# Attention units in another order: a unit's exponentials in the next unit, both halves of its squares amid that unit's score instructions, results copied out between the exponentials

## The chip, the core and the metric

The kernel runs on one core of a Trainium2 chip. The core has TensorE (matrix products; PE in the profile, and PEld for its weight loads), VectorE (DVE), ScalarE (ACT), GpSimd (POOL) and SyncE (SP, which here only issues DMAs). The metric is device time in microseconds for one execution; the median of the runs is compared.

## What is computed

Two images of 48 x 48 positions with 768 channels pass through two layers. The first is group norm, attention with decomposed relative position bias, and a projection; the second is group norm and a spectral mixing layer. The change lies in the attention of the first. Per head (12 heads of 64 channels, S = 2304 positions), cut from the reference:

```python
attn = einsum('bqc,bkc->bqk', q * scale, k)
rel_h = einsum('bhwc,hkc->bhwk', r_q, Rh); rel_w = einsum('bhwc,wkc->bhwk', r_q, Rw)
attn = softmax(attn + rel_h[..., :, None] + rel_w[..., None, :])
out = attn @ v            # then out @ proj_w + proj_b, added to x
```

All of it is float32.

## The kernel before, in words

`block_kernel` works on one image after the other: `attention`, then `project_out`, then `Spectral`. In `attention` the heads go in six pairs, both heads of a pair side by side on the partitions. The queries of a pair are cut into 18 *units* of 128 queries: six groups g, each with x = 0, 1, 2 (`order`, L481). In each iteration n of the loop (L502) the work of several units is interleaved by hand; the engines are wrapped so that every instruction keeps its place in the program (`InOrder`, L60: therefore most lines of the profile are L68). Each engine runs its own queue in that order.

One unit goes through these steps:

- `new_unit` (L346, POOL): two adds, one for each head, build the bias `s` (128 x 2304 for each head) from `rhw`, which holds the rows of the relative bias for a whole group. `s` has four buffers.
- `scores` (L360): five pieces of keys (four of 512, one of 256) by two heads, ten matmuls on TensorE into banks `ps_s`. For each, VectorE adds the product into `s` and keeps the maximum (the CUSTOM_DVE rows); then it reduces the maxima to `nm`.
- `numerators` (L389, ScalarE): four exponentials, two halves of the keys by two heads, with sums in `parts`.
- `squares` (L403, VectorE): two transposes in 32 x 32 blocks for a half, one for each head.
- `exchange` (L409): per half, six DMAs on SP's queue and two copies on ScalarE gather the blocks into `pT` (two buffers).
- `weigh` (L423): 72 matmuls on TensorE multiply `pT` with the values, into the one bank `ps_o`.
- `finish` (L440): ScalarE copies `ps_o` into `res`, VectorE sums `parts` into `dens`; at x = 2 SP stores `res`. `inverses` (L458) turns the `dens` of half a pair and sends them.

Around it stands the work that fills TensorE: in each unit of pairs 0 to 4 one piece of the next pair's keys or values (x = 0, 1) or of queries (x = 2), evicted by ScalarE (keys, queries: `by_act`) or VectorE (values: `by_dve`). Pair 5 has no next pair, so its units at x = 0 and 1 have none. The weights `w` for these come by `load_w` (L194) on SP's queue, in an iteration with x = 2 for values and keys.

The bias of a group is made ahead. At x = 2 the queries of the group after the next are projected (`queries`). One iteration later, at x = 0, `relative` (L295) multiplies them with the tables into two banks `ps_r`; ScalarE copies these to `rel`; `write` sends `rel` to DRAM with a skew (two DMAs), and `read` fetches it back straightened, as `rhw` (two DMAs). `new_unit` for that group's x = 0 unit comes two iterations after `relative`.

All banks but `ps_o` come from one pool of seven, in a ring.

The loop's order before, for iteration n (unit n is `un`, n - 1 is `last`, n - 2 is `older`): scores of un, numerators of un, a projection, weigh of older, `relative`, the evictions of ScalarE, squares and exchange of last's second half, `write`, squares and exchange of un's first half, the evictions of VectorE, `read`, finish of older, `new_unit` for n + 1.

Of the kernel before, what the change touches and what calls it, by code (L numbers as in the profile page):

```python
# [17 lines left out]
P = 128  # L18
# [144 lines left out]
def attention(tc, k, x_b, a, oT, inv_d, late, span, ps_b, ps_o):  # L163
# [12 lines left out]
    with ExitStack() as ctx:  # L176
# [65 lines left out]
        def evict(waiting):  # L242
            while waiting:
                waiting.pop(0)()
# [50 lines left out]
        def relative(g, qT):  # L295

            row0 = min(32, 40 - 8 * g)  # L300
            both = [bank(f"ps_r{h}") for h in range(2)]
            for x in range(3):
                for h in range(2):
                    r = slice(h * HD, (h + 1) * HD)
                    rows = k.rel[r, row0 : row0 + RW]
                    step = REL + 32 - 16 * x - row0
                    pe.matmul(
                        both[h][:, x * 2 * RW : (x + 1) * 2 * RW],
                        lhsT=qT[r, x, :],
                        rhs=bass.AP(rows.tensor, rows.offset, [rows.ap[0], [step, 2], [1, RW]]),  # L310
                        start=True,
                        stop=True,
                    )
            for h in range(2):
                dst = rel[:, :, :, h, :].rearrange("p k x j -> p x k j")
                src = both[h][:, :ROW].rearrange("p (x k j) -> p x k j", x=3, k=2)
                by_act.append(lambda dst=dst, src=src: act.copy(dst, src))

            rhw = qp.tile([P, 3, 2, 2 * HW], F32, tag="rhw", name="rhw")
            t_ds = []  # L320

            def write():
                for kind in range(2):
                    t_d = dp.tile([P * RS + 16], F32, tag=f"t{kind}", name=f"t{kind}")
                    t_ds.append(t_d)
                    skew = [[16 * RS + 1 - kind, 8], [RS + kind, 16], [1, ROW]]
                    sync.dma_start(
                        out=bass.AP(t_d.tensor, t_d.offset, skew),
                        in_=rel[:, kind].rearrange("p x h j -> p (x h j)"),
                    )  # L330

            def read():
                for kind, first in enumerate((47 - 8 * g - row0, 15)):
                    t_d = t_ds[kind]
                    sync.dma_start(
                        out=rhw[:, :, :, kind * HW : (kind + 1) * HW].rearrange(
                            "p x h j -> p (x h) j"
                        ),
                        in_=bass.AP(
                            t_d.tensor, t_d.offset + first, [[RS, P], [RW, 6], [1, HW]]  # L340
                        ),
                    )

            return rhw, write, read
# [11 lines left out]
            return {"pr": pr, "g": g, "x": x, "qT": qT, "s": s}  # L356

        PIECES = [(k0, min(S, k0 + 512)) for k0 in range(0, S, 512)]

        def scores(un):  # L360

            mx = smallp.tile([P, 2, len(PIECES)], F32, tag="mx", name="mx")
            for j, (k0, k1) in enumerate(PIECES):
                both = [bank(f"ps_s{h}") for h in range(2)]
                for h in range(2):
                    r = slice(h * HD, (h + 1) * HD)
                    pe.matmul(
                        both[h][:, : k1 - k0],
                        lhsT=un["qT"][r, un["x"], :],
                        rhs=kTs[un["pr"]][r, k0:k1],  # L370
                        start=True,
                        stop=True,
                    )
                for h in range(2):
                    s = un["s"][:, h, k0:k1]
                    dve.tensor_tensor_reduce(
                        out=s,
                        in0=both[h][:, : k1 - k0],
                        in1=s,
                        scale=1.0,  # L380
                        scalar=LOWEST,
                        op0=ALU.add,
                        op1=ALU.max,
                        accum_out=mx[:, h, j : j + 1],
                    )
            un["nm"] = smallp.tile([P, 2], F32, tag="nm", name="nm")
            dve.tensor_reduce(un["nm"], mx, AX.X, ALU.max, negate=True)

        def numerators(un):  # L389

            un["parts"] = smallp.tile([P, 2, 2], F32, tag="parts", name="parts")
            for half in range(2):
                for h in range(2):
                    s = un["s"][:, h, half * 2 * KQ : (half + 1) * 2 * KQ]
                    act.activation(
                        s,
                        s,
                        AF.Exp,
                        bias=un["nm"][:, h : h + 1],
                        accum_out=un["parts"][:, h, half : half + 1],  # L400
                    )

        def squares(un, half):  # L403

# [35 lines left out]
        def finish(un):  # L440

            pr, g, x = un["pr"], un["g"], un["x"]
            if x == 0:
                outs[pr, g] = outp.tile([P, 8, 3, 16], F32, tag="res", name="res")
                if g % 3 == 0:
                    dens[pr, g // 3] = outp.tile([P, 3, 2, 3], F32, tag="dens", name="dens")
            res = outs[pr, g]
            act.copy(res[:, :, x, :], un["o"][:, :P].rearrange("p (y d) -> p y d", d=16))
            dve.tensor_reduce(
                dens[pr, g // 3][:, x, :, g % 3], un["parts"], AX.X, ALU.add  # L450
            )
            if x == 2:
                sync.dma_start(
                    out=oT[pr * P : (pr + 1) * P, g * UQ : (g + 1) * UQ],
                    in_=res.rearrange("p y x d -> p (y x d)"),
                )
# [40 lines left out]
        weights[2] = load_w(2, 0)  # L497
        staged = ((0, 1), queries(0, 1))
        evict(by_act)
        recent = []  # L500
        last = turn = send = None
        for n in range(len(order) + 3):  # L502
            un = older = None
            if n < len(order):
                un = ahead
                pr, g, x = order[n]
                if g == 4 and x == 0 and pr + 1 < NP:
                    weights[0] = load_w(0, pr + 1)
                scores(un)
                recent.append(un)  # L510
            write = read = None
            if un is not None:
                numerators(un)
                ready, staged = staged, None
                if x == 2:
                    if n + 4 < len(order):
                        key = order[n + 4][:2]
                        staged = (key, queries(*key))
                    if g == 2 and pr + 1 < NP:
                        weights[2] = load_w(2, pr + 1)  # L520
                    if g == 5 and pr + 2 < NP:
                        weights[1] = load_w(1, pr + 2)
                elif n < 2:
                    for i in range(3):
                        values(0, 3 * n + i)
                    if n:
                        weights[1] = load_w(1, 1)
                elif pr + 1 < NP:
                    i = 2 * g + x
                    for j in range(0 if n == 3 else i, i + 1):  # L530
                        (keys if j < 6 else values)(pr + 1, j % 6)
            if turn is not None:
                turn()
                turn = None
            if n >= len(order) - 1 and recent:
                late(n - len(order) + 2)
            if n > 1 and recent:
                older = recent.pop(0)
                weigh(older)
            if un is not None and ready is not None:  # L540
                key, qT = ready
                rhw, write, read = relative(key[1], qT)
                groups[key] = (qT, rhw)
            evict(by_act)
            if last is not None:
                squares(last, 1)
                exchange(last, 1)
            if write is not None:
                write()
            if un is not None:  # L550
                squares(un, 0)
                exchange(un, 0)
            evict(by_dve)
            if read is not None:
                read()
            if older is not None:
                finish(older)
            if un is not None and n + 1 < len(order):
                ahead = new_unit(*order[n + 1])
            if send is not None:  # L560
                send()
                send = None
            if older is not None and older["x"] == 2 and older["g"] % 3 == 2:
                turn, send = inverses(older["pr"], older["g"] // 3)
            if len(order) - 6 <= n <= len(order):
                late()
            last = un


def shifts(t):  # L570
# [660 lines left out]
```

## Time and profile before

| | us |
|---|---|
| median of 3 runs (3729.47 to 3737.5) | 3736.94 |
| the profiled execution | 3736.53 |
| its span, first to last instruction | 3734.3 |
| TensorE busy (95%) | 3558.8 |
| VectorE busy (78%) | 2914.9 |
| ScalarE busy (68%) | 2544.2 |
| POOL busy (55%) | 2046.2 |

The profiled execution's time is 2.2 us longer than its span. The busy times are sums over the whole span. The granted TensorE clock has a mean of 0.978 of full speed. In the page's part 5 a row is a group of like instructions, with busy time, mean length of one, and the idle time of the engine just before them with what ended it. A timeline shows start, length, engine, line, operation and count of instructions in order of time; what stands in brackets is idle time before them and what ended it. In busy times by windows, each engine's busy time in a stretch stands with the count of its instructions in brackets, then the granted clock, the DMA engines' busy share and GB/s.

### The profile page before, as it was taken

How to read it: one execution, taken by the hardware profiler on the slowest of the kernel's cores; microseconds unless marked ns; L12 is line 12 of the kernel's file. 1: busy time of each engine (PE TensorE's matmuls, PEld its weight loads, DVE VectorE, ACT ScalarE, POOL GpSimd, SP SyncE). 2: the span in 40 equal slices, each digit the busy share in tenths (PEclk: the TensorE clock that was granted, in tenths of full speed). 3: DMA queues.
4: the chain of work that ended last, by engine and by line, in shares of the span. 5: the costliest groups of instructions: out<-in, count | busy, mean ns of one | idle time of the engine just before them, and what ended most of it. 6: DMA issues, size and time to landing. Idle time of an engine off the chain costs nothing.

```text
span 3734.3 us, 92576 instructions
## 1 busy us (share of the span) xinstructions
PE 3558.8 (95%) x36032; PEld 2485.7 (67%) x36032; DVE 2914.9 (78%) x6788; ACT 2544.2 (68%) x3740; POOL 2046.2 (55%) x662
## 2 busy tenths in 40 slices
PE   8999999999999888989989999999999998879899
PEld 5677776767767655566566777767677676545665
DVE  4799998989999983347657999989998999933476
ACT  3788888888888882133237888888888888821432
POOL 2566757576766663413225667575757666644232
PEclk9999999999999998999989999999999999989999
DMA  3687777778787888634526877777787778886434
GB/s 103 151 181 170 178 174 174 177 167 184 169 180 168 177 190 189 170 95 120 163 77 151 181 171 176 176 172 178 168 184 168 179 169 181 196 188 160 103 112 137
DMA packets 497859, 607.61 MB, mean 163 GB/s; under 512 B 180493, under 2 KB 312973, under 8 KB 497422
## 3 DMA queue, kind: packets, MB, share of 16 engines
q1 hardware_dynamic: 497422, 601.69, 69.0%
q8 instruction: 286, 4.69, 0.6%
q14 instruction: 151, 1.24, 0.1%
HBM read 131.61 MB, written 87.67 MB: 59 GB/s over the span
## 4 chain that ended last, share of the span: by engine, by line
PE 82%; DVE 6%; DMA 4%; ACT 4%; issue 2%; POOL 1%; SPq 1%; ACTq 0%; DVEq 0%; POOLq 0%
PE ps_o L68 21%; PE ps_s L68 20%; PE ps_proj L68 14%; PE acc L68 8%; PE ps_v L68 7%; DVE s L68 3%; PE ps L967 2%; PE ps_u L1002 2%; PE ps_y L727 2%; PE ps_r L68 2%; DMA pT<-s 2%; PE ps_x L1020 1%; SPq L68 1%; ACT pT L68 1%; PE ps_z L907 1%
## 5 line engine op out<-in xcount | busy, mean ns | idle before, releaser
L350 POOL TENSOR_TENSOR s<-rhw 128x2304 f32<-128x2304 f32 x432 | 1740.2, 4061 | 1066.8 <-DMA pT<-s 639.7
L68 DVE CUSTOM_DVE_ANT_0 s<-ps_s,s 128x512 f32<-128x512 f32 (+1 forms) x2160 | 1222.3, 633 | 312.3 <-issue 182.1
L68 ACT ACTIVATE s<-s,nm 128x1152 f32<-128x1152 f32 x864 | 1074.6, 1245 | 346.2 <-DVE nm L68 332.4
L68 DVE STREAM_TRANSPOSE s<-s 128x1152 f32<-128x1152 f32 x864 | 1111.9, 1344 | 5.5 <-ACT s L68 5.5
L68 ACT COPY pT<-s 32x1152 f32<-32x1152 f32 x864 | 993.4, 1150 | 21.7 <-PE ps_o L68 3.9
L68 PE MATMUL ps_o<-pT,v 128*64 128x128 f32 x15552 | 909.7, 277 | 65.1 <-ACT res L68 32.5
L68 PEld LDWEIGHTS ps_o<-pT,v 128*64 128x64 f32 x15552 | 877.8, 139 | 111.9 <-ACT res L68 55.8
L68 PE MATMUL ps_s<-kT,qT 64*128 64x512 f32 (+1 forms) x4320 | 899.0, 555 | 4.4 <-DVE mx L68 3.8
L68 PEld LDWEIGHTS ps_s<-kT,qT 64*128 64x128 f32 x4320 | 430.3, 187 | 418.9 <-issue 350.9
L68 PE MATMUL ps_proj<-xnT,w 128*64 128x384 f32 (+1 forms) x4032 | 589.6, 446 | 2.3 <-ACT gn_rstd L151 2.3
L68 PEld LDWEIGHTS ps_proj<-xnT,w 128*64 128x64 f32 x4032 | 280.8, 137 | 274.7 <-issue 216.9
L748 DVE TENSOR_TENSOR x<-acc,x 32x384 f32<-32x384 f32 (+2 forms) x216 | 119.2, 553 | 277.5 <-PE acc L68 194.7
L68 PE MATMUL acc<-proj 128*128 128x384 f32 x864 | 288.4, 493 | 40.8 <-POOL proj L68 40.8
L68 PE MATMUL ps_v<-w,xnT 128*64 128x128 f32 x5184 | 301.3, 276 | 0.0
L68 PEld LDWEIGHTS ps_v<-w,xnT 128*64 128x64 f32 x5184 | 285.9, 138 | 21.5 <-DVE mx L68 21.5
L68 PEld LDWEIGHTS acc<-proj 128*128 128x128 f32 x864 | 166.1, 193 | 157.5 <-POOL proj L68 41.6
L734 ACT COPY y<-ps_y 112x384 f32<-112x384 f32 x96 | 45.9, 478 | 265.8 <-PE ps_y L727 264.6
L68 POOL TENSOR_TENSOR proj<-proj 128x2304 f32<-128x2304 f32 x12 | 60.6, 5047 | 219.1 <-DMA proj<-inv_d 180.7
L68 DVE DVE_READ_ACCUMULATOR2_ANT mx<- 128x1 f32 x2160 | 179.4, 83 | 0.0
L984 POOL TENSOR_TENSOR spectrum<-spectrum 128x480 f32<-128x480 f32 x80 | 96.2, 1202 | 119.1 <-DVE spectrum L983 90.6
L68 ACT ACTIVATION_READ_ACCUMULATOR s<-s,nm 128x1 f32 x864 | 161.2, 187 | 0.0
L967 PE MATMUL ps<-w,spectrum 96*64 96x96 f32 x3200 | 143.1, 248 | 0.0
(106 smaller groups left out, 2107.1 us busy)
## 6 DMA issues: line engine op xcount, KB each, us to landing
pT<-s SPq DMA_DIRECT2D x2592, 144.0 KB
t<-rel SPq DMA_DIRECT2D x144, 189.0 KB
rhw<-t SPq DMA_DIRECT2D x144, 144.0 KB
y<-y_d SPq DMA_DIRECT2D x40, 360.0 KB
u_d<-spectrum SPq DMA_DIRECT2D x40, 360.0 KB
u<-u_d SPq DMA_DIRECT2D x48, 300.0 KB
xt<-in_x SPq DMA_DIRECT2D x12, 1152.0 KB
w<-in_qkv_w SPq DMA_DIRECT2D x36, 384.0 KB
```

The source lines that it names most:

```text
L68: return lambda *args, **kw: self.tc.keep_in_program_order(op(*args, **kw))
L350: nc.gpsimd.tensor_tensor(s[:, h, :].rearrange("p (y x) -> p y x", x=HW), rhw[:, x, h, :HW][:, :, None].to_broadcast([P, HW, HW]), rhw[:, ...
L727: nc.tensor.matmul(ps[:YP, : 2 * SC], lhsT=k.fw, rhs=part[:, t0 : t0 + 2, ch], start=True, stop=True,)
L734: nc.scalar.copy(y1[:, :, ch], ps[:YP, : 2 * SC].rearrange("p (t c) -> p t c", c=SC))
L748: nc.vector.tensor_tensor(dst, acc[p : p + n, :UQ], dst, ALU.add)
L907: nc.tensor.matmul(ps[:BS, w * 96 : (w + 1) * 96], lhsT=self.y2[s, j][:, w, i * BS : (i + 1) * BS], rhs=k.fh, start=True, stop=True,)
L967: nc.tensor.matmul(ps[64 * r : 64 * r + 64, w * BS : (w + 1) * BS], lhsT=self.o1[:, ri, f0 : f0 + 64], rhs=w2[:, (0, 2, 1, 0)[2 * r + ri], ...
L984: nc.gpsimd.tensor_tensor(val, val, clip, ALU.subtract)
L1002: nc.tensor.matmul(ps[: 2 * HW, :480], lhsT=k.ih, rhs=d2[:, c0 : c0 + 480], start=True, stop=True)
L1020: nc.tensor.matmul(ps[: 2 * HW, : 2 * SC], lhsT=k.iw, rhs=self.u2[s, i][:, t : t + 2, :], start=True, stop=True,)
```

## The change

For iteration n there are now four units in work: `un` = n, `last` = n - 1, `older` = n - 2 and `weighed` = n - 3. The new order is: numerators of last, first half; finish of weighed; `write` (with the two `rel` copies of ScalarE, which stood in `relative` before); numerators of last, second half; scores of un, pieces 0 to 2; squares and exchange of last, both halves; `read`; scores of un, pieces 3 and 4, with the reduction to `nm`; then the loads and the projection, weigh of older, `relative`, the evictions, `new_unit`. `write` and `read` belong to the `relative` of the iteration before. `finish` comes an iteration after `weigh`, and its sum for `dens` goes to VectorE's evictions. The inverses follow an iteration later, and the last ones stand behind the loop.

```diff
 def relative(g, qT):
-            for h in range(2):
-                dst = rel[:, :, :, h, :].rearrange("p k x j -> p x k j")
-                src = both[h][:, :ROW].rearrange("p (x k j) -> p x k j", x=3, k=2)
-                by_act.append(lambda dst=dst, src=src: act.copy(dst, src))
...
             def write():
+                for h in range(2):
+                    act.copy(
+                        rel[:, :, :, h, :].rearrange("p k x j -> p x k j"),
+                        both[h][:, :ROW].rearrange("p (x k j) -> p x k j", x=3, k=2),
+                    )
...
+        EARLY, REST = (0, 1, 2), (3, 4)
+        def scores(un, pieces):
...
+        def numerators(un, half):
...
-            dve.tensor_reduce(
+            by_dve.append(lambda: dve.tensor_reduce(
                 dens[pr, g // 3][:, x, :, g % 3], un["parts"], AX.X, ALU.add
-            )
+            ))
...
+        for n in range(N + 3):
+            un, last, older, weighed = (units.get(n - i) for i in range(4))
+            if n < N:
+                un = units[n] = ahead
+            if last is not None:
+                numerators(last, 0)
+            if weighed is not None:
+                finish(weighed)
+            if write is not None:
+                write()
+            if last is not None:
+                numerators(last, 1)
+            if un is not None:
+                scores(un, EARLY)
+            if last is not None:
+                for half in range(2):
+                    squares(last, half)
+                    exchange(last, half)
+            if write is not None:
+                read()
+                write = read = None
+            if un is not None:
+                scores(un, REST)
             if un is not None:
                 pr, g, x = order[n]
+                ready, staged = staged, None
                 if g == 4 and x == 0 and pr + 1 < NP:
                     weights[0] = load_w(0, pr + 1)
...
+            if older is not None:
                 weigh(older)
             if un is not None and ready is not None:
                 key, qT = ready
                 rhw, write, read = relative(key[1], qT)
                 groups[key] = (qT, rhw)
             evict(by_act)
-            if last is not None:
-                squares(last, 1)
-                exchange(last, 1)
-            if write is not None:
-                write()
-            if un is not None:
-                squares(un, 0)
-                exchange(un, 0)
             evict(by_dve)
-            if read is not None:
-                read()
-            if older is not None:
-                finish(older)
...
+            if weighed is not None and weighed["x"] == 2 and weighed["g"] % 3 == 2:
+                turn, send = inverses(weighed["pr"], weighed["g"] // 3)
...
+        turn()
+        evict(by_act)
+        send()
```

## The prediction

> **What bounds the kernel now.** I read the page first (TensorE 95% busy, the chain of waits 82% TensorE), then the busy time by windows, to see in which stage that share holds. Attention takes about 1335 us of each image's 1867 us and runs six pairs of heads of 18 units. Columns: window, its length, busy PE, PEld, DVE, ACT, POOL, granted clock, DMA share, GB/s.
>
> ```profile
> 752.00:973.00 221.00, 221.00 (x2492) 156.94 (x2488) 199.51 (x477) 189.16 (x260) 143.75 (x36) 1.00 0.77 174
> 1195.00:1412.00 217.00, 185.13 (x1833) 132.17 (x1830) 194.33 (x465) 183.22 (x249) 140.29 (x35) 0.94 0.83 183
> ```
>
> The first is pair 3: TensorE is busy 221.00 of 221.00 us. Pairs 0 to 4 are like it, 221.5 us each (the distances between the units' `nm` reductions repeat 12.05, 12.69, 12.02 us). No step there can become faster unless TensorE gets less to do, and the change leaves its work as it is; every wait the change puts on TensorE lengthens the run. The second is pair 5, whose units at x=0 and x=1 have no projection to fill TensorE: 185 of 217 us busy. Only there (2 x 217 us) is something to be had. VectorE needs 10.88 us for a unit (the shortest distance of two `nm`), so at best 2 x (217 - 18 x 10.88) = 42 us.
>
> So I looked for cover that is lost, in the order of time over one group of three units (x=1, x=2, then x=0 of the next group). Columns: start, us, engine, line, operation, count. TensorE, SP, POOL and VectorE:
>
> ```profile
> 841.75 4.03 PE L68 MATMUL ps_s<-kT,qT 64*128 64x512 f32 x20
> ...
> 853.66 4.14 PE L68 MATMUL ps_s<-kT,qT 64*128 64x512 f32 x20
> ...
> 865.71 4.14 PE L68 MATMUL ps_s<-kT,qT 64*128 64x512 f32 x20
> ```
> ```profile
> 842.82 1.31 SPq L68 DMA_DIRECT2D t<-rel  x2
> 844.32 4.21 SPq L68 DMA_DIRECT2D pT<-s  x6
> 848.57 1.85 SPq L68 DMA_DIRECT2D rhw<-t  x2
> 851.33 7.75 SPq L68 DMA_DIRECT2D pT<-s  x12
> 859.37 0.35 SPq L68 DMA_DIRECT2D oT<-res  x1
> 859.76 0.45 SPq L197 DMA_DIRECT2D w<-in_qkv_w  x1
> ```
> ```profile
> 854.24 24.15 POOL L350 TENSOR_TENSOR s<-rhw 128x2304 f32<-128x2304 f32 x6 [11.06 <-ACT s L68]
> ```
> ```profile
> 866.96 0.69 DVE L68 CUSTOM_DVE_ANT_0 s<-ps_s,s 128x512 f32<-128x512 f32 x1 [1.08 <-POOL s L350]
> ...
> 867.58 0.69 DVE L68 CUSTOM_DVE_ANT_0 s<-ps_s,s 128x512 f32<-128x512 f32 x1
> ```
>
> The reader is to see a chain: SP issues the `rhw` reads at 848.57, 6.8 us after the scores of the x=1 unit begin (841.75). POOL, idle for 11.06 us, starts at 854.24, 5.7 us after the issue (the bracket names ACT, but SP's reads landed at 853.8 by their semaphores). It builds `s` of the coming x=0 unit in two adds of 4.06 us (24.15 / 6 is 4.03 a step), done at 862.3. VectorE's second score instruction of that unit, the first that needs the second head, runs at 867.58. **The chain has 5.2 us to spare.**
>
> **The change, part by part.** The count of instructions stays; all costs are of order.
>
> *SP.* Both exchanges of a unit (12 copies) now stand between the `t` writes and the `rhw` reads, where one exchange of 6 stood, and each half waits for its squares, which now stand after six score instructions. From the scores' start: first score instruction at 1.25 (866.96 - 865.71), six at 0.61 end at 4.9, two squares (four take 5.15 in this timeline, so 2.6) at 7.5, 12 copies at 7.75 / 12 = 0.65 end at 15.3. The reads go out at 15.3 in place of 6.8: 8.5 us later against 5.2 to spare, so `s` is **3.3 us late** once a group. VectorE stands at the second score instruction of the x=0 unit; behind it wait all its others, and TensorE, which needs the bank of the fourth score for its projection (banks go round in a ring of seven; the first projection matmul follows that score's end even now). In pairs 0 to 4 TensorE loses it in full.
>
> *The bias banks.* `rel` is copied out by ScalarE in the next unit, behind two exponentials and the copy of the result. From the x=0 unit's start: VectorE's `nm` at 1.25 + 3.7 + 5.15 + 1.9 + 0.2 = 12.2; ScalarE's last `pT` copies end at 10.1 + 2 x 1.15 = 12.4, the `kT` copy (units with keys) at 13.0; two exponentials of 1.25, 0.27 and 0.48 make 16.3 (15.7 without `kT`). The next unit's scores start at 12.7, and their sixth tile, now due at 1.8 after that, gets the bank of the first `rel` copy: it waits 1.8 us (1.2 without `kT`). This wait and the late `s` are not added: a unit x=1 that is 1.8 us longer gives the chain from the reads 1.8 us more. Only what the sixth score delays VectorE's squares adds: due at 4.3, there at 3.6 + 1.0, so 0.4 us with keys, none with values. **A group costs 3.3 to 3.7; I take 3.5.**
>
> *Weights.* `w` for values and keys is loaded at an x=2 unit and used by the next unit's projection. Now it is issued at 859.76, 6.1 after the scores' start; then it comes behind the 12 copies, at 15.3, and lands 4.1 later (median of the 36 loads by their semaphores, most from 3.3 to 5.8), at 19.4. The projection is due at 12.05 + 4.07 = 16.1: a wait of 3.3 us, of which some 1.7 are already in the group's 3.5, so 1.6 more; nine loads an image (five of values, four of keys).
>
> *What is hidden.* Exponentials: `nm` to the first squares is 6 us of ScalarE work beside VectorE's six scores and the second half's beside the first squares (ScalarE 189 of 221 us). If this cover went, VectorE would stand at the squares, 2.5 us a unit at most. Weights times values: `pT` lands at 7.5 + 11 x 0.65 + 4 = 18.7, needed at 12.05 + 8.1 = 20.1; 1.4 us of cover remain. The result's copy is early now and frees `ps_o`: this takes away pair 5's waits for `res` (2.9 us each), after which VectorE is next. The `dens` sums (0.12), the `oT` stores and the inverses a unit later wait for nobody. VectorE and POOL overlap in another phase: their operations last 1.33 to 1.38 (transposes) and 4.05 to 4.07 us (adds) wherever they fall now, so nothing, at most those 0.05 us each.
>
> *Pair 5.* The same chain closes over VectorE: from the first score of x=1, 14.1 to the reads, 5.7, two adds 8.1, then the other 10.3 us of the unit: 38.2, with up to 1.4 for the held bank 39.6, against 217 / 6 = 36.2 a group now. I take 39: 5 groups x 2.8 = 14 us lost, so the pair's gain is gone.
>
> *The clock.* A wait of 2.90 us of TensorE ahead of 1216.14 was followed by this (window, length, PE; the granted clock stands before the DMA share):
>
> ```profile
> 1213.20:1216.20 3.00, 0.10 (x3) 0.06 (x3) 2.96 (x14) 2.84 (x4) 1.28 (x1) 1.00 0.70 210
> 1216.80:1220.20 3.40, 3.40 (x36) 3.40 (x34) 3.40 (x4) 3.40 (x7) 0.00 (x0) 0.50 1.13 188
> ```
>
> Half clock for 3.4 us costs up to 1.7. Four of the five 2.9 us waits of that pair show it, the 1.5 us ones don't. The new waits of about 3.3 us are 36 (18 loads, 18 groups after them), broken by matmuls in between: from none to 36 x 1.7 = 61; I take 25.
>
> The Trainium skill (TensorE: Matmul & The Clock Gate, Part 1, "What's actually happening") has the clock fall after at least one idle window of about 3.4 us. By that rule alone no wait of 3.3 us would count and the sum would be 25 us less; the row above shows a shorter wait that did.
>
> **The sum.** Per image 28 groups (30 of pairs 0 to 4 less the first two, whose units last 13 to 20 us) x 3.5 = 98, loads 9 x 1.6 = 14, pair 5 14: 126. Twice 252, clock 25: 277. The profiled execution took 3736.5 us (span 3734.3), 0.4 below the median 3736.94, so 4013, said as **4010**. Bounds: the 5.7 us from read to POOL rests on reads that land 3.6 to 6.9 us after issue, so -1 to +1.2 in 66 groups (-65 to +80); loads 3.3 to 5.8, -15 to +30; clock -25 to +36. Alone it would be 3905 to 4155.
>
> **Rivals.** (a) *Only banks and loads bite*: reads land early enough. Against it: 12 copies at 0.65 can't go out sooner. Then per pair 2 x 3.3 + 2 x 1.8 + 2 x 1.2 = 12.6; 2 x 4.7 pairs: about +120, 3860. (b) *Faster*: pair 5 falls to VectorE's 10.88 us a unit and nothing is late; -42 gives 3695. Place: x=0 and x=1 units of pair 5; it decides if `s` is ready by the second score instruction, for which the reads must go out within 6.8 + 5.2 = 12 us of the x=1 scores. For it: VectorE's 194 of 217 us there, and the waits for `res`. Against it: 15.3. (c) *The exchange is late too*: `pT` lands past 20.1 because the 16 DMA engines (share 0.77) get 12 copies in a row; 0.7 us in 180 units more gives 4140. (d) *No change*: all waits fall into time that TensorE makes up; its 221 of 221 speaks against; 3737.
>
> **How the numbers follow.** Forecast 0.72, (a) 0.12, (b) 0.05, (c) 0.08, (d) 0.03. The range 3850 to 4150 takes in the forecast, (a) and (c) but for their far sides. Faster by over 0.2% (what a measurement of this kernel can tell from no change) 0.05, within 0.2% 0.03, slower 0.92.
>
> **What would show it.** Right: reads behind 12 copies; POOL's long idle time before each x=0 unit ended by them; VectorE waiting some 2 to 3 us for `s` after the first score of x=0 units; TensorE waiting for ACT's `rel` at x=1 and for the `w` load; TensorE's share near 89%; no `ps_o` wait for `res`. Wrong: TensorE still 221 of 221 in pair 3, or an unnamed wait in each unit and not each group.

## The result, and the profile after

The changed kernel takes **4047.74 us** (median of 4 runs, 4045.66 to 4054.39) against 3737.22 for the kernel before, run beside it: a ratio of 1.0837, 95% interval 1.0816 to 1.0858. The forecast was 4010, the range 3850 to 4150. The profiled execution took 4054.39 us, its span is 4052.5, and the mean granted clock fell from 0.978 to 0.953.

TensorE's busy time rises although its work is the same (x36032 in both), and the chain that ended last leaves TensorE (82% of it before). First row of part 1 and of part 4 of the page after:

```profile
PE 3746.7 (92%) x36032; PEld 2584.8 (64%) x36032; DVE 2925.8 (72%) x6788; ACT 2521.9 (62%) x3740; POOL 2044.0 (50%) x662
```
```profile
PE 39%; DVE 25%; DMA 11%; SPq 8%; POOL 7%; issue 6%; ACT 4%; POOLq 0%; ACTq 0%; DVEq 0%
```

Busy time by windows after, pair 3 and pair 5 of the first image (columns as in the prediction):

```profile
837.00:1085.00 248.00, 235.27 (x2498) 163.28 (x2498) 200.68 (x475) 187.52 (x261) 143.68 (x37) 0.97 0.68 156
1332.00:1575.00 243.00, 204.27 (x1857) 140.75 (x1851) 198.92 (x473) 183.93 (x252) 141.37 (x36) 0.92 0.73 171
```

Pair 3 took 221 us with TensorE busy throughout; now it takes 248, with 13 us idle and 14 us of slower matmuls: the same matmuls are busy for 235.27 in place of 221.00, at a granted clock of 0.97. Pair 5 takes 243 in place of 217.

The chain that the prediction followed, in the changed kernel. SyncE from the writes of `rel` in the unit g2 x=1 of pair 3 (its scores begin at 934.85) to the load of `w` in g3 x=0 (scores at 960.69), and POOL:

```profile
938.69 1.31 SPq L68 DMA_DIRECT2D t<-rel  x2
942.92 8.43 SPq L68 DMA_DIRECT2D pT<-s  x12
951.39 1.26 SPq L68 DMA_DIRECT2D rhw<-t  x2
952.75 0.48 SPq L68 DMA_DIRECT2D oT<-res  x1
956.35 7.69 SPq L68 DMA_DIRECT2D pT<-s  x12
964.08 0.59 SPq L197 DMA_DIRECT2D w<-in_qkv_w  x1
```
```profile
955.87 24.14 POOL L350 TENSOR_TENSOR s<-rhw 128x2304 f32<-128x2304 f32 x6 [15.70 <-DMA oT<-res]
```

Twelve copies stand ahead of the reads, and twelve ahead of the load. POOL is idle for 15.70 us and starts when the reads have landed (955.6 by their semaphores). The bracket names the store of `res`, the DMA issued next; the add doesn't use that store. SyncE ahead of the x=0 unit of g1 (the reads that this unit needs), then VectorE and TensorE in it; its scores begin at 878.60:

```profile
862.27 7.79 SPq L68 DMA_DIRECT2D pT<-s  x12
870.11 1.26 SPq L68 DMA_DIRECT2D rhw<-t  x2
```
```profile
879.86 0.69 DVE L68 CUSTOM_DVE_ANT_0 s<-ps_s,s 128x512 f32<-128x512 f32 x1 [0.74 <-PE ps_s L68]
...
883.59 0.69 DVE L68 CUSTOM_DVE_ANT_0 s<-ps_s,s 128x512 f32<-128x512 f32 x1 [3.03 <-POOL s L350]
```
```profile
878.60 3.70 PE L68 MATMUL ps_s<-kT,qT 64*128 64x512 f32 x16
884.35 1.31 PE L68 MATMUL ps_s<-kT,qT 64*128 64x256 f32 x4 [2.04 <-DVE mx L68]
885.58 5.79 PE L68 MATMUL ps_proj<-xnT,w 128*64 128x384 f32 x24
...
938.35 2.41 PE L68 MATMUL ps_s<-kT,qT 64*128 64x512 f32 x10 [0.77 <-ACT rel L68]
940.69 4.09 PE L68 MATMUL ps_proj<-xnT,w 128*64 128x384 f32 x24
```

TensorE at the load, g3 x=0:

```profile
964.73 1.31 PE L68 MATMUL ps_s<-kT,qT 64*128 64x256 f32 x4 [0.34 <-DVE mx L68]
968.12 5.62 PE L68 MATMUL ps_v<-w,xnT 128*64 128x128 f32 x72 [2.08 <-DMA w<-in_qkv_w]
```

VectorE has the first score, waits 3.03 us for the second head's `s`, and TensorE waits for the bank behind it. At 938.35 is the wait for the `rel` copy at x=1, at 968.12 the wait for the load. And here stands what the prediction sized worst: the projection behind the 2.04 us takes 5.79 us, and 4.09 elsewhere. The stretch behind those 2.04 us, by windows (the granted clock stands before the DMA share):

```profile
884.34:886.00 1.66, 1.65 (x6) 0.79 (x8) 1.66 (x5) 0.39 (x2) 1.66 (x1) 0.95 0.00 0
886.00:890.90 4.90, 4.90 (x24) 1.92 (x20) 4.90 (x8) 1.57 (x2) 4.90 (x2) 0.67 0.07 16
```

The matmuls run on half clock for about 3.4 us of these. Over the execution the time at half clock is 380 us, and was 165 before.

Where the time went, from the distances between the `nm` reductions, both images added (us):

| | before | after | difference |
|---|---|---|---|
| pair 0 | 456.6 | 505.0 | +48.4 |
| pairs 1 to 4 | 1771.6 | 2009.2 | +237.6 |
| pair 5 | 436.6 | 482.1 | +45.5 |
| last `nm` of image 1 to first of image 2, and behind the last of image 2 | 989.7 | 976.4 | -13.3 |

### The profile page after: what moved, and what is told of

Same layout as the page of the kernel before. It is cut to its first block, busy times and chain, and to the rows that moved or that the text cites. A ratio compares the mean times of both kernels' runs of the same rounds, so it can differ in the third digit from the quotient of the medians.

```text
span 4052.5 us, 92619 instructions
## 1 busy us (share of the span) xinstructions
PE 3746.7 (92%) x36032; PEld 2584.8 (64%) x36032; DVE 2925.8 (72%) x6788; ACT 2521.9 (62%) x3740; POOL 2044.0 (50%) x662
## 4 chain that ended last, share of the span: by engine, by line
PE 39%; DVE 25%; DMA 11%; SPq 8%; POOL 7%; issue 6%; ACT 4%; POOLq 0%; ACTq 0%; DVEq 0%
DVE s L68 22%; SPq L68 8%; PE ps_o L68 7%; PE acc L68 7%; DMA pT<-s 6%; PE ps_v L68 6%; POOL s L350 6%; PE ps_s L68 5%; PE ps_proj L68 5%; PE ps L977 2%; PE ps_u L1012 2%; PE ps_y L737 1%; ACT s L68 1%; DMA w<-in_qkv_w 1%; DMA oT<-res 1%
## 5 line engine op out<-in xcount | busy, mean ns | idle before, releaser
L350 POOL TENSOR_TENSOR s<-rhw 128x2304 f32<-128x2304 f32 x432 | 1738.1, 4059 | 1396.3 <-DMA oT<-res 759.4
L68 DVE CUSTOM_DVE_ANT_0 s<-ps_s,s 128x512 f32<-128x512 f32 (+1 forms) x2160 | 1239.7, 630 | 617.4 <-PE ps_s L68 265.7
L68 PE MATMUL ps_s<-kT,qT 64*128 64x512 f32 (+1 forms) x4320 | 999.7, 565 | 135.5 <-DVE mx L68 108.1
L68 PE MATMUL ps_o<-pT,v 128*64 128x128 f32 x15552 | 914.5, 278 | 34.7 <-DMA pT<-s 15.8
L68 PEld LDWEIGHTS ps_s<-kT,qT 64*128 64x128 f32 x4320 | 460.4, 188 | 613.9 <-issue 279.9
L68 PE MATMUL ps_proj<-xnT,w 128*64 128x384 f32 (+1 forms) x4032 | 620.0, 463 | 15.3 <-DMA w<-in_qkv_w 13.0
L68 PEld LDWEIGHTS ps_proj<-xnT,w 128*64 128x64 f32 x4032 | 292.8, 142 | 307.7 <-issue 239.6
L68 PE MATMUL ps_v<-w,xnT 128*64 128x128 f32 x5184 | 349.7, 303 | 24.2 <-DMA w<-in_qkv_w 14.3
L68 PEld LDWEIGHTS ps_v<-w,xnT 128*64 128x64 f32 x5184 | 334.5, 155 | 49.2 <-DVE mx L68 27.7
```

The source lines that it names most:

```text
L68: return lambda *args, **kw: self.tc.keep_in_program_order(op(*args, **kw))
L350: nc.gpsimd.tensor_tensor(s[:, h, :].rearrange("p (y x) -> p y x", x=HW), rhw[:, x, h, :HW][:, :, None].to_broadcast([P, HW, HW]), rhw[:, ...
```

## The experiments

The theory is that order on SyncE's queue sets the time: reads, then loads, come behind twelve copies, `s` is late, and TensorE pays in waits and in clock. The rival is that the squares amid the scores hold banks, whatever SyncE does.

**Each wait taken away by itself.** First the reads, put between the two halves of the exchange:

```diff
                 for half in range(2):
                     squares(last, half)
                     exchange(last, half)
-            if write is not None:
-                read()
-                write = read = None
+                    if half == 0 and write is not None:
+                        read()
+                        write = read = None
```

> The changed kernel with one line moved: the rhw reads go out between the two halves of the exchange, behind 6 copies and not behind 12. Theory (the late reads, the held bias banks and the late weight loads cost, by the order of SP's queue): the reads stand at about 11.4 us after the scores' start, s is ready about 0.6 us before it is needed, and only banks and loads are left: 12.6 us a pair in pairs 0 to 4, a half-rate clock after the load waits, pair 5 near its old time. Expected 3870 us (3830 to 3910). Rival (the squares amid the scores keep VectorE from freeing the banks, since the profile names the maxima mx as what TensorE's ps_s waits for): the squares stay where they are, so no change, 4030 to 4070.

Measured 3942.96 us, 1.0558 (1.0539 to 1.0576): 105 us come back, though not the 180 expected. The rival falls as the cause of these waits: the squares stay amid the scores, and TensorE's waits for `mx` ahead of scores fall from 108.1 us in all to 5.4. Part of what is left is waits for the loads (64.8 us in all, 27.3 in the changed kernel). The load for g3 of pair 3 goes out 4.0 us after its unit's scores (3.4 in the changed kernel), since the unit itself starts earlier. TensorE there:

```profile
934.64 6.80 PE L68 MATMUL ps_v<-w,xnT 128*64 128x128 f32 x72 [4.26 <-DMA w<-in_qkv_w]
941.26 4.11 PE L68 MATMUL ps_o<-pT,v 128*64 128x128 f32 x72
```

The wait is 4.26 us now, and the projection behind it takes 6.80 us, mostly on half clock (granted clock 0.59 over it). Another wait has grown as well, that of `weigh` for `pT`, which was 15.8 us in all (in all, times, longest):

```profile
PE ps_o L68 <- DMA pT<-s: 76.3, 46, 10.6
```

Next the `rel` copies, put back where they were:

```diff
 def relative(g, qT):
+            for h in range(2):
+                dst = rel[:, :, :, h, :].rearrange("p k x j -> p x k j")
+                src = both[h][:, :ROW].rearrange("p (x k j) -> p x k j", x=3, k=2)
+                by_act.append(lambda dst=dst, src=src: act.copy(dst, src))
...
             def write():
-                for h in range(2):
-                    act.copy(
...
```

> The changed kernel with the two rel copies back in the iteration of relative, at ScalarE's evictions. Theory: the wait for the bias banks at x=1 vanishes, but it was time that the chain from the reads had for nothing; without it s is late by the full 3.3 us in each group, so only some 0.2 us a group are won and longer single waits may bring the half-rate clock more often: 4020 to 4070. Rival (the held banks are a cost of their own): 1.2 to 1.8 us in each of 66 groups saved, about 3950.

Measured 4037.37 us, 1.0804 (1.0784 to 1.0825), an interval that overlaps the changed kernel's. By itself this wait costs next to nothing, since the late `s` that it shares its time with remains. Third, the loads of values and keys, ahead of the exchange:

```diff
+                if x == 2 and g == 2 and pr + 1 < NP:
+                    weights[2] = load_w(2, pr + 1)
+                if x == 2 and g == 5 and pr + 2 < NP:
+                    weights[1] = load_w(1, pr + 2)
                 scores(un, EARLY)
...
-                    if g == 2 and pr + 1 < NP:
-                        weights[2] = load_w(2, pr + 1)
-                    if g == 5 and pr + 2 < NP:
-                        weights[1] = load_w(1, pr + 2)
```

> The changed kernel with the weight loads of values and keys issued ahead of the unit's exchange and not behind it. Theory: the 18 load waits of 3.3 us go, but in those groups the late s is what is left, so 18 x 1.6 us and part of the half-rate clock after them are won: 3995 to 4030. Rival (the loads are a cost of their own): 18 x 3.4 us and 18 x 1.6 us of half-rate clock, about 3955.

Measured 3987.88 us, 1.068 (1.0649 to 1.0711): 60 us back, more than the theory's 18 to 53. With the load waits went 100 us of half clock (380 to 280).

**All three together.**

> The changed kernel with all three: reads between the halves, rel copies at home, loads ahead of the exchange. The exponentials in the next unit, the squares amid the scores and the early copy of the result stay. Theory: nothing of the loss is left in pairs 0 to 4 (221.5 us each again), and pair 5 keeps its gain, up to 20 us an image: 3700 to 3745. Rival (the new order of exponentials, squares and results costs by itself, by banks held or pT landing late): 3800 or more.

Measured 3831.34 us, 1.025 (1.0234 to 1.0267): 216 of 310 us are back; the expectation of 3700 to 3745 was wrong, and its rival (3800 or more) came true. Scores, reads and loads are all in time now; TensorE's largest wait is the one that the changed kernel hardly had. Waits (in all, times, longest):

```profile
PE ps_o L68 <- DMA pT<-s: 116.4, 67, 10.7
...
DVE s L68 <- POOL s L350: 29.0, 4, 22.9
```

This is the late `pT` of the prediction's rival (c), by another cause than it gave: the two reads stand among the copies now. In pairs 1 to 4 the last copy of an x=0 unit goes out 4.8 us after the x=2 unit's scores (median; 3.0 in the changed kernel), and `weigh`, due at 8.0, mostly starts at 8.4 to 9.7. The 1.4 us of cover that the prediction named are used up.

**Is it SyncE's queue or the DMA engines?** The reads of that version issued by ScalarE, between its own copies for `pT`:

```diff
-                    sync.dma_start(
+                    act.dma_start(
```

> The kernel with all three corrections, and the rhw reads issued on ScalarE's queue between its copies of the two halves instead of on SP's. Theory: what was left (1829 us for pairs 1 to 4 of both images against 1772) is pT landing late in the unit after the reads, because the two reads take 1.3 us of SP's queue ahead of the second half; without them there the pairs return to 1772 to 1790 us, and the time to 3760 to 3790. Rival (the 16 DMA engines are what is full, not SP's queue): the reads move the same bytes, so 3820 to 3840.

Measured 3822.70 us, 1.0232 (1.0211 to 1.0253). The theory named there (issue time on SyncE) falls: without the reads in SyncE's queue the last copy goes out at 4.4 us in place of 4.8 (medians as above), and the copies still land late:

```profile
PE ps_o L68 <- DMA pT<-s: 83.7, 44, 9.1
```

The Trainium skill (DMA: Bandwidth & Descriptors, "Issuing engines are not separate DMA queues") says that starting DMAs from several engines saves only the issuing engine's own time. The 9 us between these two medians agree. The time lies in the rival's range, but no run here isolates the 16 DMA engines, so that they are what is full isn't shown.

**Earlier squares instead.** The three moves, and the squares after four score instructions:

```diff
-        EARLY, REST = (0, 1, 2), (3, 4)
+        EARLY, REST = (0, 1), (2, 3, 4)
```

> The kernel with all three corrections, and the squares after two pieces of the scores (four VectorE instructions) and not three. Theory: squares and copies stand 1.2 us earlier, pT lands in time again, pairs 1 to 4 fall from 1829 us to 1775 to 1790, and pair 5, which waits for pT too, gains some 10 us an image: 3745 to 3785. Rival (the second half's exponentials end only 6 to 7 us after the scores' start, so the squares wait for them instead): 3815 to 3835.

Measured 3778.24 us, 1.0118 (1.0103 to 1.0133), as the theory had it. The exchange begins 1.2 us earlier, and in pairs 1 to 4 `weigh` finds `pT` nearly always. What remains there sits in two units of each pair; TensorE of such a unit (scores at 804.63):

```profile
808.70 4.09 PE L68 MATMUL ps_proj<-xnT,w 128*64 128x384 f32 x24
814.14 0.28 PE L68 MATMUL ps_i<-ident,inv 128*18 128x128 f32 x1 [1.35 <-DVE mx L68]
814.56 4.15 PE L68 MATMUL ps_o<-pT,v 128*64 128x128 f32 x72
```

The transpose of the inverses needs a bank; seven back in the ring is that of the fifth score, which now stands behind the squares. The next version issues it behind `weigh`, and the one after that also keeps three early pieces in the first four units:

```diff
-            if turn is not None:
-                turn()
-                turn = None
...
                 weigh(older)
+            if turn is not None:
+                turn()
+                turn = None
```
```diff
+            EARLY, REST = ((0, 1), (2, 3, 4)) if n > 3 else ((0, 1, 2), (3, 4))
```

> The version before this one (reads between the exchange halves, rel copies at home, loads early, squares after two pieces: 3778) with one more move: the transpose of the inverses (ps_i) is issued behind weigh in place of ahead of it. In that version's trace weigh starts at 9.93 in place of 7.99 in two units of each pair, those with this transpose: seven banks back from ps_i is that of the fifth score, which now stands behind the squares (score ends at 9.4). Theory (the ring of banks): weigh starts at 7.99 there again, pairs 1 to 4 fall from 1802 to 1772 to 1778, 20 such units by 1.9 us give 3735 to 3750. Rival (the transpose waits for the inverses themselves, or TensorE only moves the wait to the next unit): 3765 to 3785.

> As e9_turn, and the squares stand after three pieces again in the first four units of each image, where three projections in a row need the banks of the fourth to sixth score. Theory (banks): the first distances of nm, 21.7, 17.5 and 22.0, come back toward 18.2, 16.0 and 20.4, 13 us over both images: 3722 to 3738. Rival (these units are long for another reason, the exponentials a unit later): no change against e9_turn.

Measured 3762.03 us, 1.0075 (1.0061 to 1.0089), and 3754.86 us, 1.0053 (1.0040 to 1.0066), 12 and 17 us above what was expected. In the first, `weigh` of that unit starts 7.99 us after its scores, as expected (scores at 803.84), yet pairs 1 to 4 got only 12.6 us faster (1801.9 to 1789.3) where some 27 were expected. TensorE of the first version, that unit:

```profile
811.83 4.10 PE L68 MATMUL ps_o<-pT,v 128*64 128x128 f32 x72
815.86 0.28 PE L68 MATMUL ps_i<-ident,inv 128*18 128x128 f32 x1
```

And its x=2 unit of g4 in pair 2:

```profile
726.17 4.15 PE L68 MATMUL ps_o<-pT,v 128*64 128x128 f32 x72 [1.31 <-DMA pT<-s]
```

Part of the freed time returns as a wait for `pT` in the unit behind a load of `w`: of the 17.7 us that pairs 1 to 4 still take above the kernel before, 8.5 lie in this place, and the rest is spread over other units. That the units ahead now leave the transfers less time is argued, not shown. In the second, pair 0 got 10 us faster (475.2 to 465.0) of the 13 expected, and pair 5 gave back 5.6 of them.

**The reads alone, in the kernel before.** Everything as before, but the reads stand behind the next exchange of six copies:

```diff
                 squares(last, 1)
                 exchange(last, 1)
+            if late_read is not None:
+                late_read()
+                late_read = None
...
-            if read is not None:
-                read()
+            late_read = read
```

> The kernel before, with the rhw reads alone put behind the next unit's first 6 copies. Theory: they go out 6.6 us later (at 855.2 and not at 848.57 in the timeline of before), 5.2 are to spare, so s is 1.4 us late in each of some 66 groups: 3735 + 92, with no half-rate clock since 1.4 us is short: 3800 to 3860. Rival (the reads have room enough, the loss came with the exponentials and squares): 3730 to 3745.

Measured 3805.53 us, 1.0191 (1.0168 to 1.0214): one moved pair of DMAs costs 71 us (3805.53 - 3805.53 / 1.0191) with no other part of the change, 1.1 us a group in 66 groups. The expectation had no half clock, since waits of 1.4 us were called short, but 12 of the 72 units x=0 show it (2 in the kernel before). The waits are the same as in the changed kernel:

```profile
DVE s L68 <- POOL s L350: 141.6, 80, 22.5
...
PE ps_s L68 <- DVE mx L68: 37.9, 29, 2.9
```

**What half clock costs.** First, ten extra matmuls into the projection's bank, overwritten by it, in the load waits:

```diff
+        def warm(ps):
+            for i in range(5):
+                for h in range(2):
+                    pe.matmul(
+                        ps[h * HD : (h + 1) * HD, :UQ],
...
             ps = bank("ps_proj")
+            if fill:
+                warm(ps)
```

> The changed kernel, with 10 extra matmuls (3.2 us) into the projection's own bank, overwritten by it, in 16 of the 18 units whose projection waits for a weight load. Theory: they fit into the wait of 3.4 us, so they cost nothing, and TensorE stays busy, so that the projection after the wait runs at the full clock: some 40 us of the 42 lost there come back, 3995 to 4020, by more work. Rival (the half-rate clock is not the wait's doing): nothing gained, up to 16 x 0.5 us lost, 4040 to 4060.

Measured 4045.38 us, 1.0824 (1.0804 to 1.0845): inconclusive. The edit fills all 18 units, and the extra matmuls themselves wait for the bank of the late fourth score. In g3 of pair 3 they end 1.0 us after the load has landed (7.91 of the unit); the projection starts at 8.94 in place of 7.44 and takes 4.10 us (full clock) in place of 5.62: the same end. In 9 of the 18 units the extra matmuls run on half clock themselves, as in g0 of pair 3 behind a wait of 2.89 us:

```profile
842.62 5.84 PE L68 MATMUL ps_proj<-xnT 128*64 128x384 f32 x20
848.29 4.04 PE L68 MATMUL ps_proj<-xnT,w 128*64 128x384 f32 x24
```

The second attempt fills the other wait, from a bank that is free, with the eighth score's matmul issued four more times:

```diff
+                again = 4 if j == 3 and un["x"] == 0 and un["g"] % 3 < 2 else 0
-                for h in range(2):
+                for h in (0, 1) + (1,) * again:
```

> The changed kernel, and in four of six units x=0 (g 0, 1, 3, 4) the matmul of the eighth score is issued four more times into its own bank, about 1.7 us, in the wait of some 2 us ahead of the ninth score; the result is the same. Theory (half clock after these waits costs its own time): units x=0 at half clock fall from 51 to under 25, and each returns 1.6 to 2 us: 3965 to 4010. Rival (the half clock lies beside other waits that take its place): 4035 to 4060, though the half-clock time falls.

Measured 4009.62 us, 1.0745 (1.0726 to 1.0764). With 96 extra matmuls in an image the kernel is 38 us faster. Units x=0 with half clock fall from 51 to 16 of 72, the half-clock time from 380 to 205 us. TensorE in the unit shown above, with the repeats (x28 in place of x20):

```profile
866.74 7.57 PE L68 MATMUL ps_s<-kT,qT 64*128 64x512 f32 x28
874.24 4.09 PE L68 MATMUL ps_proj<-xnT,w 128*64 128x384 f32 x24
```

No gap, and the projection takes 4.09 us where it took 5.79. The repeats take 3.4 us of TensorE here (eight records 0.43 us apart), not the expected 1.7, and reach past the wait: the projection starts 7.50 us after the unit's scores (6.98 without them) and still ends 1.2 us earlier. The time is at the very end of the theory's 3965 to 4010 and clear of the rival's 4035 to 4060: half clock costs time of its own, some 0.2 us for each of the 175 us that went, with the repeats' own time already taken off.

**The one part that helps, alone.** The kernel before, with only the copy of the result (the `act.copy` of `finish`, now a function `take`) moved ahead of ScalarE's copies for `pT`:

```diff
             evict(by_act)
+            if older is not None:
+                take(older)
             if last is not None:
                 squares(last, 1)
```

> The kernel before, with one move alone: ScalarE copies the result of weigh right after the projection's copies, ahead of the squares' own copies to pT, in place of behind them; exponentials, squares, exchanges, reads and loads stay. In the trace before, weigh in pair 5 waits 2.9 us for this copy (five times in an image), and four of these waits are followed by half clock. Theory (pair 5 is held by this bank): the waits go and so do their half clocks, and pair 5 loses 5 x 2 to 4 us in each image, down to VectorE's pace at the least: 3695 to 3720, pairs 0 to 4 unchanged. Rival (the transfer of pT or VectorE is due at the same time): 3728 to 3740.

Measured 3727.08 us against 3735.92, 0.998 (0.9972 to 0.9989): **faster than both kernels**, if by less than the theory said. Pairs 0 to 4 stay (456.9 and 1771.7), pair 5 falls from 436.6 to 422.7 and its half-clock time from 51 to 20 us; 20 of the 34 distances of `nm` within it are now VectorE's 10.9 us (12 before). ScalarE and TensorE of this version in pair 5:

```profile
1210.87 0.26 ACT L68 COPY res<-ps_o 128x128 f32<-128x128 f32 x1
1211.14 4.65 ACT L68 COPY pT<-s 32x1152 f32<-32x1152 f32 x4
```
```profile
1210.66 2.41 PE L68 MATMUL ps_s<-kT,qT 64*128 64x512 f32 x10 [1.01 <-ACT rel L68]
1213.84 4.15 PE L68 MATMUL ps_o<-pT,v 128*64 128x128 f32 x72 [0.77 <-DMA pT<-s]
```

The copy came 5 us later before (1215.82), and `weigh` waited 2.90 us for it; now it waits 0.77 for `pT`. Of the 13.9 us some 4 are lost behind the attention, where the stages are 4.2 us longer in all.

## Why the prediction was right, and where it was off

The sign, the place and the mechanism are as predicted; it came out 38 us low. Inside pairs 0 to 4 two terms missed in opposite directions and made up for each other, which is luck.

- **SyncE and the late `s`.** Predicted: reads at 15.3 us of the x=1 scores, `s` 3.3 us late. In pair 3 they go out at 15.4 (870.11, scores of g0 x=1 at 854.67), and the second score instruction of g1 x=0, which waits for them, runs 3.1 us late (883.59 - 878.60 = 4.99, before 1.87). Over pairs 0 to 4 the medians are 16.1 for the reads and 2.7 for the lateness. Shown as cause both ways: undone it gives 105 us, done alone it costs 71.
- **Bias banks.** Predicted 1.8 us, not to be added to the late `s`. The sixth tile runs at 3.50 in place of 1.72 in g2 of pair 3, but the wait isn't there once a group, as the prediction had it: 14 of the 60 units x=1 in pairs 0 to 4 have it, and 10 of the 12 in pair 5. Taking it away alone gives 10 us or nothing. That group takes 40.39 us where it took 36.90: 3.49, the predicted 3.5. It is one of the cheaper ones: of the 56 groups that the sum counts, the 14 with neither a load nor half clock are 2.6 to 4.9 us longer, 4.05 on average.
- **Loads.** Predicted a wait of 3.3 us: the projection runs 7.43 us after its scores (968.12 - 960.69) where 4.07 was due, so 3.4. The run without these waits gave 60 us where the sum had 28, but 17 of the 18 groups with a load show half clock, and the 60 us hold it. In the run with the filled waits 44 of the 56 groups have no half clock; they are 3.97 us longer on average, and the 17 of them with a load 3.88. So a load adds nothing of its own there, where 1.6 was predicted (29 us too much in all), and a group costs some 0.5 more than 3.5 (26 us too little).
- **The clock: the term that was mis-sized.** The prediction took 25 us, with 0 to 61 as bounds, and counted only waits near 3 us. Waits of 2 us were often enough, and 51 of the 72 units x=0 show half clock. The trace before already has a wait of 2.46 us in pair 5 that half clock follows (at 1399.77). The filled waits returned 38 us; half of the 215 us by which half-clock time grew, 108, is the most it can be if matmuls take twice their time on half clock. So it lies between 38 and 108.
- **Pair 5.** Predicted 28 us lost in both images, measured 45.5. Half-clock time grew by 31 us there, up to 15 us of the 17.5.
- **Pairs 0 to 4** lost 286 us, 278 of them in the 56 groups of the sum. Predicted were 224 before the clock; 56 groups at the 3.97 us of the filled run's full-clock groups make 222. The remaining 56 us are then the clock's there (an estimate), against 25.
- **Behind the attention** the changed kernel is 13 us faster; the prediction had no such term, and no run here was aimed at it.
- **What was said to be hidden.** The cover of 1.4 us for `pT` held in the changed kernel (waits of 15.8 us in all), but it was the next limit: with the reads early it was gone at once. The waits of `weigh` for `res` are gone, as predicted; alone this part is worth 9 us.
- **My expectation for the three moves together** (3700 to 3745) was wrong by 86 us at the least, since it took the transfers behind the reads to be hidden.

## What to carry to other kernels

A DMA that starts a long chain (here two reads, two adds and all scores of three units) should be looked at by its place in the issuing queue, not by its size: twelve copies put ahead of it cost more than any other part that was undone by itself. When a wait is taken away, ask at once which transfer or bank was hidden by it; here a load, `pT` and a bank came up one behind the other. And a change that helps one stage may be worth taking out of its parcel: the copy of the result, by itself, is a gain.

## What the runs showed of the hardware

- Half clock follows shorter waits than expected, and not all of them: one wait of 2.04 us was followed by some 3.4 us of half clock, another of 1.97 us (g5 of pair 3) was not. The Trainium skill (TensorE: Matmul & The Clock Gate, Part 1, "What's actually happening") puts the fall after at least one idle window of about 3.4 us, windows that run freely. The 2.04 us do not agree with this as a length of wait. By that rule only three waits in the units x=0 of pairs 0 to 4 (3.66, 3.72 and 3.98 us) would have cost clock, and the filled waits of about 2 us, worth 38 us, show that shorter ones did.
- Matmuls that do nothing useful can pay: in the unit shown four repeats in place of a wait of 2.04 us made the next projection start 0.5 us later and last 1.7 us less (5.79 to 4.09).
- The releaser that a trace names can be a neighbour: all 44 of POOL's waits put down to the store of `res` (759.4 us) end 0.2 to 0.8 us after the reads issued just ahead of it land.
